# GpSimd products of a selective scan over four quarters at once, halo copies on ScalarE, and new task durations in the planner

## The chip, the core and the metric

The kernel runs on one core of a Trainium2 chip. The core has five engines that work through queues of their own: TensorE (PE, matrix products into PSUM), VectorE (DVE), ScalarE (ACT, functions from tables), GpSimd (POOL) and SyncE (SP, which here issues the DMA transfers). The metric is the device time of one execution in microseconds (us); the median of the runs counts. Traces come from one profiled execution, which has a time of its own.

## The reference

An image batch of 2 x 256 channels x 64 x 64 pixels goes through two residual layers, each after a group normalisation: a Mamba block with a feed-forward part, and attention with 8 heads over all 4096 pixels. The change concerns the scan of the Mamba block:

```python
proj = u @ W_xp.T
dt = softplus(proj[..., :R] @ W_dt.T + b_dt)
Bm, Cm = proj[..., R:R + N], proj[..., R + N:]
A = -exp(A_log)

def step(h, inp):
    dt_t, B_t, C_t, u_t = inp
    dA = exp(dt_t[:, :, None] * A)
    h = dA * h + (dt_t * u_t)[:, :, None] * B_t[:, None, :]
    return (h, einsum('bdn,bn->bd', h, C_t))
```

There are 512 inner channels (DI), N = 16 states for each and R = 16. u is the output of a causal convolution of 4 taps along the pixels and a SiLU. Before the scan stand a layer norm and the input projection; after it a gate, an output projection, a GELU feed-forward layer and the residual sum. All values are 32-bit floats.

## The kernel before

**Tiles and steps.** The Mamba layer comes first, in `mamba_stage`, and the attention follows it. The 4096 pixels of each of the 2 images are cut into 8 tiles of T = 512 columns, so there are 16 tiles. The 512 inner channels are 4 blocks (index k) of 128. A tile's scan has 32 steps: 4 blocks k, times 4 groups of states qd, times 2 values of `quarter` (0 and 2). Rows in a step are 32 channels times 4 states; a block's 128 channels fall into four quarters of 32, and one step handles two of them, j = 0 and 1, that is quarters `quarter` and `quarter + 1`. Two steps that follow each other, with `quarter` 0 and 2, are a pair: all four quarters of one block and one group of states. In all there are 512 steps, 256 pairs and 1024 scan instructions.

**One step** (function `step`, from L808) adds these tasks:

- ACT, twice: `decay` (L828), da = exp(dt * A), into a buffer in SBUF (da0) for j = 0 and in PSUM (da1) for j = 1.
- PE: `broadcast_b`, which spreads the four rows of B over the 128 rows of a PSUM tile bn.
- The product dt*u*B for j = 1, called dbu1 (`times_b`, L834). In three steps of four (`pooled`, g % 4 != 3) it is made by POOL, from dtu_rep and from rows of B in SBUF (rows_b, tile b); in the fourth by DVE, from dtu_rep and bn.
- DVE: the product for j = 0 (L834 too), from dtu_rep and bn, written over bn.
- DVE, twice: `scan` (L839), tensor_tensor_scan of da and the product, starting from `state`, into one half of h.
- ACT: `keep` (L842), a copy of the last column of h into `state`.
- POOL: `times_c` (L845), h times the row of C, 1024 columns wide.
- PE, once a pair: `add_up` (L869, L871) sums h over the states into y; at the last group of states DVE multiplies y by the gate z (L881).

dt and dt*u are made per block k in `softplus` (PE, ACT, DVE, then three POOL instructions of 512 columns at L614, L615 and L617), stored to DRAM, and loaded again spread over the rows as dt_rep and dtu_rep (`load_rep`, L792), two quarters at a time, 512 KB each. The convolution (`conv`) needs the last three columns of the tile before it: POOL copies them from `halo` into xm (L581) and the new ones from xm into `halo` (L583). Around the scan run the work before it for the next tile (`front`), after it for the last (`back`), and from the ninth tile on the attention's projections for the first image (`qkv`).

**What sets the order.** No order is written out by hand. Each task is added to a planner (class `Plan`) with its engine, a due step, a cost in us, what it reads and writes, and for a DMA a time until it lands. `Plan.order` plays all engines forward with these costs: an engine that is free takes the ready task with the smallest due step, if its buffers have room. ACT functions of another table set are ranked 6 steps later (SWITCH), and a table load counts 1.3 us. The order that comes out is emitted and is fixed in the program; on the chip each engine goes through its own list in that order and waits by semaphores. The costs thus change no instruction's length, only the order.

**Buffers.** A `Ring` hands out a number of buffers of one name in turn. `Plan.room` says whether a task's new buffers are free at the planned moment. Of those that matter here there are 4 buffers of two quarters each for dt_rep and for dtu_rep, 3 of da0, 2 of da1, 2 of bn (PSUM), 3 of dbu1, and 5 of h.

Of the kernel before, what the change touches and what calls it, by code (L numbers as in the profile page):

```python
# [107 lines left out]
class Plan:  # L108
# [60 lines left out]
    def room(self, task, now):  # L169
        for buf in task.bufs:  # L170
            ring = buf.ring
            if not ring or buf.given:
                continue
            if not ring.free and len(ring.given) < buf.turn:
                return False
            if len(ring.given) >= ring.bufs:
                old = ring.given[-ring.bufs]
                if old.left or old.free > now:
                    return False
        return True  # L180
# [78 lines left out]
def mamba_stage(ctx, tc, xs, stats_out, consts, w, outs, scratch):  # L259
# [51 lines left out]
    r_dtr, r_dtur = ring("dt_rep", 4, 2, pool=sc), ring("dtu_rep", 4, 2, pool=sc)  # L311
    r_b, r_c = ring("b", NQ, pool=sc), ring("c", NQ, pool=sc)
    r_da0, r_da1 = ring("da0", 3, pool=sc), ring("da1", 2, pool=ps)
    r_bn, r_dbu1 = ring("bn", 2, pool=ps), ring("dbu1", 3, pool=sc)
# [174 lines left out]
    def front(i):  # L489
# [12 lines left out]
        for k in range(KC):  # L502
            add("ACT", due - 41, 0.75, lambda k=k: norm(k), [yn[k], scales_buf[b * KC + k]], [yn[k]])
# [3 lines left out]
        add("PE", due - 40, 1.8, lambda: matmul(mean.tile, [(lnmat, yn.tile[:, k, :]) for k in range(KC)]), [yn], [mean])  # L507
        sq = [Buf(r_tmp) for _ in range(KC)]
        var = Buf(mm)
        for k in range(KC):  # L510

            def centre(k=k):
                nc.vector.tensor_sub(yn.tile[:, k, :], yn.tile[:, k, :], mean.tile)

            add("DVE", due - 39, 0.7, centre, [mean], [yn[k]])
            square = lambda k=k: nc.scalar.activation(sq[k].tile, yn.tile[:, k, :], AF.Square)
            add("ACT", due - 38, 0.65, square, [yn[k]], [sq[k], var] if k == 0 else [sq[k]])
# [6 lines left out]
        add("PE", due - 37, 1.9, lambda: matmul(var.tile, [(lnmat, s.tile) for s in sq]), sq, [var])  # L524
        add("ACT", due - 36, 1.25, rstd, [], [var], ("exp",))
        for k in range(KC):

            def scale(k=k):
                y = yn.tile[:, k, :]
                nc.vector.scalar_tensor_tensor(y, y, gamma[:, k : k + 1], var.tile, ALU.mult, ALU.mult)  # L530

            def shift(k=k):
                y = yn.tile[:, k, :]
                nc.scalar.activation(y, y, AF.Identity, bias=beta[:, k : k + 1])  # L534

            add("DVE", due - 35, 0.75, scale, [var], [yn[k]])
            add("ACT", due - 34, 0.75, shift, [], [yn[k]])
# [19 lines left out]
        add("PE", due - 14, 3.6, project, d.u, [pp, proj, bc])  # L557
        add("ACT", due - 13, 0.6, lambda: nc.scalar.copy(proj.tile[:NP, :], pp.tile[:NP, :]), [pp], [proj])
        add("ACT", due - 13, 0.6, lambda: nc.scalar.copy(bc.tile, pp.tile[:NP, :]), [pp], [bc])
        add("SP", due - 12, 0.4, store_bc, [bc], [d.bc], lands=1.6)  # L560
        add("DVE", due - 12, 0.7, halves, [pp, proj], [proj])
# [4 lines left out]
    def conv(d, b, k, due):  # L566

        px, pc, xm = Buf(mm), Buf(mm), Buf(r_xm, 2)
        h = halo_buf[b * KD + k]

        def project():
            matmul(px.tile, [(w_in[:, c, bass.ts(k, P)], d.yn.tile[:, c, :]) for c in range(KC)])

        def convolve():
            matmul(pc.tile, [(taps[:, k, j, :], xm.tile[:, j : j + T]) for j in range(TAPS)])

        def silu():
            nc.scalar.activation(d.u[k].tile, pc.tile, AF.Silu, bias=conv_b[:, k : k + 1])

        add("PE", due, 1.8, project, [d.yn], [px, xm])  # L580
        add("POOL", due, 0.2, lambda: nc.gpsimd.tensor_copy(xm.tile[:, 0:HALO], halo[:, b, k, :]), [h], [xm[0]])  # L581
        add("ACT", due + 1, 0.6, lambda: nc.scalar.copy(xm.tile[:, HALO:], px.tile), [px], [xm[1]])
        add("POOL", due + 2, 0.2, lambda: nc.gpsimd.tensor_copy(halo[:, b, k, :], xm.tile[:, T:]), [xm], [h])  # L583
        add("PE", due + 2, 3.6, convolve, [xm], [pc, d.u[k]])
        add("ACT", due + 4, 0.6, silu, [pc], [d.u[k]], ("silu",))

    def softplus(d, k, due):
# [22 lines left out]
        add("PE", due, 0.8, lambda: matmul(pd.tile, [(w_dt[:, i, bass.ts(k, P)], d.proj.tile) for i in range(2)]), [d.proj], [pd, dt, lw])  # L610
        add("ACT", due + 1, 1.95, exps, [], [pd, dt], ("exp",))
        add("ACT", due + 1, 1.2, logs, [pd], [lw, w1], ("exp",))
        add("DVE", due + 2, 0.7, rest, [pd], [w1])
        add("POOL", due + 3, 1.27, lambda: nc.gpsimd.tensor_sub(lw.tile, lw.tile, w1.tile), [w1], [lw])  # L614
        add("POOL", due + 3, 1.27, lambda: nc.gpsimd.tensor_add(dt.tile, dt.tile, lw.tile), [lw], [dt])  # L615
        add("SP", due + 3.5, 0.9, lambda: store(d.dt[k], dt, "dt_dram"), [dt], [d.dt[k]], lands=2.0)
        add("POOL", due + 3.5, 1.27, lambda: nc.gpsimd.tensor_mul(lw.tile, dt.tile, d.u[k].tile), [dt, d.u[k]], [lw])  # L617
        add("SP", due + 4, 0.9, lambda: store(d.dtu[k], lw, "dtu_dram"), [lw], [d.dtu[k]], lands=2.0)

    def gate(d, k, due):  # L620
# [7 lines left out]
        add("PE", due, 1.8, project, [d.yn], [pz, z])  # L628
        add("ACT", due + 1, 0.6, lambda: nc.scalar.activation(z.tile, pz.tile, AF.Silu), [pz], [z], ("silu",))

    def back(i):
# [5 lines left out]
        for m in range(KC):  # L637
# [7 lines left out]
            for k in range(0, KD, 2):  # L645
                reads = d.z if k == 0 else d.z[k : k + 2]
                add("PE", due + 2 * m, 1.9, lambda k=k, project=project: (project(k), project(k + 1)), reads, [po])
# [3 lines left out]
                0.7,  # L651
# [7 lines left out]
        for f in range(KH):  # L659
# [8 lines left out]
            add("PE", due + 5 + 1.5 * f, 1.9, up, [yn], [ph, hid if f == 0 else hid[f]])  # L668
            add("ACT", due + 6 + 1.5 * f, 0.7, gelu, [ph], [hid[f]], ("gelu",))
        for m in range(KC):  # L670
# [10 lines left out]
            for f in range(0, KH, 2):  # L681
                reads = [hid, yn[m]] if f == 0 else [hid[f], hid[f + 1]]
                add("PE", due + 19 + 4 * m + f / 2, 2.7 if f == 0 else 1.8, lambda f=f, down=down: down(f), reads, [acc])
# [6 lines left out]
            add("DVE", due + 24 + 4 * m, 1.45, end, [acc], [xt[m], stats_bufs[IMAGES + b][m * NT + t]])  # L690
# [3 lines left out]
    def qkv(b, t, due):  # L694
# [25 lines left out]
        for k in range(KC):  # L720
            add("ACT", due + 2, 0.75, lambda k=k: norm(k), [hid[3 + k], scales_buf[(IMAGES + b) * KC + k]], [hid[3 + k]])
        for n, (i, m) in enumerate(((1, 0), (1, 1), (0, 0), (0, 1))):
# [21 lines left out]
            add("PE", at, 1.8, project, [hid[k] for k in range(5)], [pm, *halves])  # L744
            add("ACT", at + 0.5, 0.7, high, [pm], [hid[5]])
            add("DVE", at + 1, 0.7, low, [pm, hid[5]], [hid[6]])
            add("SP", at + 1.5, 1.7, store, halves, [], lands=3.3)
        for j in range(0, T // P, 2):
# [16 lines left out]
            add("PE", at, 1.8, project, [hid[k] for k in range(5)], [pv, hid[7]])  # L765
            add("ACT", at + 0.5, 0.7, lambda pv=pv: nc.scalar.copy(hid.tile[:, 7, :], pv.tile), [pv], [hid[7]])
# [14 lines left out]
    def pooled(g):  # L781

        return g % 4 != 3

    def load_rep(g, name, src, ring_):

        i, k, _, quarter = where(g)
        rep = Buf(ring_, 2)

        def load():  # L790
            rows = src.tile.rearrange("(c j) t -> c (j t)", j=QUAD)[:, quarter * T : (quarter + 2) * T]
            nc.sync.dma_start(rep.tile, rows.unsqueeze(1).to_broadcast([PQ, QUAD, 2 * T]))  # L792

        add("SP", g - 7, 1.7, load, [src], [rep], lands=3.3)
        return rep
# [13 lines left out]
    def step(g):  # L809
# [4 lines left out]
        if qd == 0:  # L814
            d.dtu_rep[quarter] = load_rep(g, "dtu_rep", d.dtu[k], r_dtur)
            d.dt_rep[quarter] = load_rep(g, "dt_rep", d.dt[k], r_dtr)
# [3 lines left out]
        dt, dtu, rows_b, rows_c = d.dt_rep[quarter], d.dtu_rep[quarter], d.b[qd], d.c[qd]  # L820
        states = [((b * KD + k) * QUAD + quarter + j) * NQ + qd for j in range(2)]
        da = [Buf(r_da0), Buf(r_da1)]
        bn, dbu1 = Buf(r_bn), Buf(r_dbu1)
# [9 lines left out]
        def times_b(engine, out, j, rows):  # L833
            engine.tensor_mul(out.tile, dtu.tile[:, j, :], rows.tile)  # L834

        def scan(j):
            dbu = dbu1 if j else bn
            initial = state[:, b, k, quarter + j, qd : qd + 1]
            nc.vector.tensor_tensor_scan(h.tile[:, j, :], da[j].tile, dbu.tile, initial, ALU.mult, ALU.add)  # L839
# [7 lines left out]
        for j in range(2):  # L847
            add("ACT", g - 6 + j, 0.71, lambda j=j: decay(j), [dt[j]], [da[j]], ("exp",))
        add("PE", g - 6, 0.4, broadcast_b, [d.proj], [bn])
        if pooled(g):  # L850
            add("POOL", g - 6, 1.27, lambda: times_b(nc.gpsimd, dbu1, 1, rows_b), [dtu[1], rows_b], [dbu1])
        else:
            add("DVE", g, 0.7, lambda: times_b(nc.vector, dbu1, 1, bn), [dtu[1], bn], [dbu1])
        add("DVE", g, 0.7, lambda: times_b(nc.vector, bn, 0, bn), [dtu[0]], [bn])
        for j, dbu in ((1, dbu1), (0, bn)):
            add("DVE", g, 1.27, lambda j=j: scan(j), [da[j], dbu, state_buf[states[j]]], [h[j]])
        add("ACT", g - 6, 0.25, keep, [h], [state_buf[at] for at in states])
        add("POOL", g - 4, 2.36, times_c, [rows_c], [h])
# [20 lines left out]
        add("PE", g - 3, 1.9 if qd == 0 else 1.1, add_up, [s.h for s in pair] + ([d.u[k]] if qd == 0 else []), [y])  # L879
        if qd == NQ - 1:  # L880
            add("DVE", g + 2.5, 0.7, lambda: nc.vector.tensor_mul(d.z[k].tile, y.tile, d.z[k].tile), [y], [d.z[k]])  # L881
# [9 lines left out]
    for i, d in enumerate(tiles):  # L891
        d.z, d.b, d.c, d.dt_rep, d.dtu_rep = [], [], [], {}, {}
# [568 lines left out]
```

## Time and profile before

| | |
|---|---|
| median of 3 runs | 4506.31 us (4498.84 to 4507.3) |
| profiled execution, span | 4505.2 us |
| PE busy over the span | 4257.1 us (94%) |
| DVE busy | 3890.9 us (86%) |
| ACT busy | 3768.4 us (84%) |
| POOL busy | 3807.4 us (85%) |
| first and last scan (start) | 96.9 and 2060.8 us |
| first logits of the attention | 2115.5 us |
| activation-table loads, whole program | 332 of 1283 ns |

The span is one execution from its first to its last instruction on the one core. The Mamba layer takes its first 2115.5 us and the attention the rest. In the group lines that follow, a line is: source line, engine, operation, output <- inputs, shape and count, then busy us and mean ns of one instruction, then how long the engine stood idle just before such instructions, and what ended that idle time. Times of instructions that follow each other on an engine overlap a little in the trace, so the distance from one start to the next is somewhat shorter than the duration.

### The profile page before, as it was taken

What the parts mean: (1) busy time and instruction counts of PE and PEld (TensorE: products, weight loads), DVE (VectorE), ACT (ScalarE), POOL (GpSimd) and SP (SyncE); (2) the same over time, 40 slices, a digit from 0 to 9 for tenths busy, and PEclk for the clock granted to TensorE, in tenths of its full rate; (3) what the DMA queues carried; (4) which work ended last, traced back from release to release, by engine and by line L of the source; (5) the groups of instructions that cost most, each with busy time, mean ns of one, the idle gap of its engine ahead of it and who ended that gap; (6) DMA issues with size and microseconds to landing.
All of it is one profiled execution on the core that took longest, in us unless ns stands there. A gap on an engine that the chain in (4) does not pass through costs nothing.

```text
span 4505.2 us, 53942 instructions
## 1 busy us (share of the span) xinstructions
PE 4257.1 (94%) x18530; PEld 1642.2 (36%) x18530; DVE 3890.9 (86%) x3309; ACT 3768.4 (84%) x4842; POOL 3807.4 (85%) x2249
## 2 busy tenths in 40 slices
PE   5789999999999999988999999999999999999998
PEld 2233333333333333333333333333353333333333
DVE  4999999999999989894888888888848888888888
ACT  4788888888788889873999999999849999999997
POOL 2999999999999999994788888888728888888886
PEclk8899999999999999999999999999999999999999
DMA  5233333333443434445210140101091110401100
GB/s 192 94 120 101 110 125 122 127 127 127 143 148 134 139 126 140 147 153 144 58 27 17 29 101 17 26 17 30 24 265 35 46 26 17 101 17 29 27 19 8
DMA packets 172281, 389.23 MB, mean 86 GB/s; under 512 B 23392, under 2 KB 49760, under 8 KB 163808
## 3 DMA queue, kind: packets, MB, share of 16 engines
q1 hardware_dynamic: 171120, 383.37, 27.4%
q8 instruction: 147, 2.41, 0.2%
q10 hardware_dynamic: 880, 2.36, 0.2%
q14 instruction: 134, 1.10, 0.1%
HBM read 292.33 MB, written 93.32 MB: 86 GB/s over the span
## 4 chain that ended last, share of the span: by engine, by line
PE 57%; DVE 4%; ACT 3%; POOL 3%; issue 2%; DMA 1%; DVEq 0%; POOLq 0%; SPq 0%; ACTq 0%
PE s L1131 25%; PE po L1161 24%; PE mm L444 3%; DVE h L839 2%; POOL h L845 2%; ACT da L828 1%; ACT L244 1%; PE mm L677 1%; PE s L1016 1%; PE y L871 1%; POOL dbu L834 1%; PE sums_ps L1212 1%; DVE bn L834 1%; PE mm L641 0%; PE bn L444 0%
## 5 line engine op out<-in xcount | busy, mean ns | idle before, releaser
L1153 DVE TENSOR_REDUCE chunk<-chunk 128x1024 f32<-128x4096 f32 x288 | 1270.6, 4412 | 242.4 <-ACT chunk L1144 242.3
L1194 POOL TENSOR_TENSOR acc_p<-acc_p,e 128x1024 f32<-128x1024 f32 x480 | 1151.9, 2400 | 196.7 <-ACT e L1144 178.0
L1144 ACT ACTIVATE chunk<-s 128x1024 f32<-128x1024 f32 x992 | 1121.5, 1131 | 185.5 <-PE s L1131 139.9
L845 POOL TENSOR_TENSOR h<-h,c 128x1024 f32<-128x1024 f32 x512 | 1208.5, 2371 | 42.0 <-ACT state L842 28.9
L1131 PE MATMUL s<-q,k 128*128 128x512 f32 x4096 | 1228.4, 422 | 5.8 <-ACT chunk L1144 4.9
L1161 PE MATMUL po<-chunk,v 128*32 128x512 f32 x3968 | 1121.7, 642 | 0.0
L1161 PE MATMUL po<-e,v 128*32 128x512 f32 x4224 | 1080.0, 605 | 0.0
L1144 ACT ACTIVATE e<-s 128x1024 f32<-128x1024 f32 x1056 | 1072.7, 1019 | 7.4 <-PE s L1131 6.9
L1131 PEld LDWEIGHTS s<-q,k 128*128 128x128 f32 x4096 | 691.3, 188 | 1014.4 <-issue 915.0
L828 ACT ACTIVATE da<-dt_rep,neg_a 128x512 f32<-128x512 f32 x1024 | 690.5, 701 | 128.7 <-DVE h L839 106.0
L1192 POOL TENSOR_TENSOR acc_p<-acc_p,e 128x512 f32<-128x512 f32 x480 | 620.2, 1292 | 129.3 <-ACT e L1144 106.6
L839 DVE TENSOR_TENSOR_SCAN h<-da,state,dbu 128x512 f32<-128x512 f32 x512 | 650.5, 1273 | 42.8 <-POOL dbu L834 40.2
L839 DVE TENSOR_TENSOR_SCAN h<-da,state,bn 128x512 f32<-128x512 f32 x512 | 647.1, 1264 | 11.6
L834 POOL TENSOR_TENSOR dbu<-dtu_rep,b 128x512 f32<-128x512 f32 x384 | 488.5, 1283 | 19.7 <-DMA dtu_rep<-dtu_dram 15.0
L244 ACT ACT_TABLE_LOAD x332 | 426.0, 1283 | 6.7 <-PEq L1451 0.7
L444 PE MATMUL bn<-proj,pick 112*128 112x512 f32 x512 | 296.4, 595 | 112.2 <-DVE h L839 111.6
L871 PE MATMUL y<-h,sum 128*32 128x512 f32 x2048 | 359.1, 635 | 42.2 <-POOL h L845 42.1
L834 DVE TENSOR_TENSOR bn<-dtu_rep,bn 128x512 f32<-128x512 f32 x512 | 348.6, 681 | 41.4 <-PE bn L444 27.8
L1191 DVE TENSOR_TENSOR acc<-acc,e 128x512 f32<-128x512 f32 x448 | 310.7, 694 | 30.9 <-ACT e L1144 17.5
L1161 PEld LDWEIGHTS po<-chunk,v 128*32 128x32 f32 x3968 | 144.3, 108 | 361.5 <-issue 349.9
L444 PE MATMUL mm<-yn,w_in 128*128 128x512 f32 x512 | 254.7, 625 | 10.3 <-ACT yn L534 9.1
L444 PE MATMUL mm<-yn,w 128*128 128x512 f32 x512 | 246.5, 611 | 4.2 <-ACT hid L666 2.1
(143 smaller groups left out, 4016.3 us busy)
## 6 DMA issues: line engine op xcount, KB each, us to landing
dt_rep<-dt_dram SPq DMA_DIRECT2D x128, 512.0 KB, 5.1
dtu_rep<-dtu_dram SPq DMA_DIRECT2D x128, 512.0 KB, 5.7
k<-qk_dram SPq DMA_DIRECT2D x62, 512.0 KB, 7.3
q<-qk_dram SPq DMA_DIRECT2D x124, 256.0 KB, 4.7
b<-bc_dram SPq DMA_DIRECT2D x64, 256.0 KB, 3.0
c<-bc_dram SPq DMA_DIRECT2D x64, 256.0 KB, 3.7
dt_dram<-dt SPq DMA_DIRECT2D x64, 256.0 KB, 2.0
dtu_dram<-lw SPq DMA_DIRECT2D x64, 256.0 KB, 2.3
```

Of the source, the lines that this page charges most:

```text
L244: self.nc.scalar.preload_act_table_set(self.TABLES[task.table])
L444: nc.tensor.matmul(out, lhsT=lhsT, rhs=rhs, start=(i == 0), stop=(i == len(pairs) - 1))
L828: nc.scalar.activation(da[j].tile, dt.tile[:, j, :], AF.Exp, scale=scale)
L834: engine.tensor_mul(out.tile, dtu.tile[:, j, :], rows.tile)
L839: nc.vector.tensor_tensor_scan(h.tile[:, j, :], da[j].tile, dbu.tile, initial, ALU.mult, ALU.add)
L845: nc.gpsimd.tensor_tensor(h.tile, h.tile, rows_c.tile.unsqueeze(1).to_broadcast([P, 2, T]), ALU.mult)
L1131: nc.tensor.matmul(ps[:, j, :], lhsT=keys[i // NT, kt][:, h, kj : kj + P], rhs=queries[i][:, h, :], start=True, stop=True)
L1144: nc.scalar.activation(e, todo[s].s[half], AF.Exp, scale=SCALE)
L1153: nc.vector.tensor_reduce(out, terms, AX.XY, ALU.add)
L1161: nc.tensor.matmul(tiles[i].po[h * D : (h + 1) * D, :], lhsT=v[:, c, g * P + h * D : g * P + (h + 1) * D], rhs=todo[s].e[h // 2][:, h % 2, :],
L1192: nc.gpsimd.tensor_add(acc_p[:, 1, :], acc_p[:, 1, :], eb[:, 1, :])
L1194: nc.gpsimd.tensor_add(acc_p, acc_p, eb)
```

## The change

1. `pooled` now decides by the pair: 11 of every 16 pairs have their dbu1 products on POOL, spread evenly; before, 3 of 4 single steps had. A pooled pair's two products (quarters 1 and 3) are one POOL instruction of 1024 columns, `both_times_b`, issued in the pair's first step. In the other pairs DVE makes both, one in each step, from bn.
2. So that one instruction can read both quarters, dtu_rep becomes 2 buffers of four quarters (QUAD = 4), filled by two loads of two quarters each, and dbu1 becomes 2 buffers of two products. dt_rep stays as it was. The loads are issued in the order dtu 0 and 1, dt 0 and 1, dtu 2 and 3, then in the next step dt 2 and 3.
3. The two halo copies of `conv` move from POOL to ACT.
4. Nearly all task costs of the planner are replaced by shorter ones.
5. `Plan.room` counts the buffers that a task takes from a ring one by one, so a task that takes two from the same ring is handled.

```diff
     def room(self, task, now):
+        taken = {}
         for buf in task.bufs:
...
-            if not ring.free and len(ring.given) < buf.turn:
+            n = taken[ring] = taken.get(ring, -1) + 1
+            if not ring.free and len(ring.given) + n < buf.turn:
                 return False
-            if len(ring.given) >= ring.bufs:
-                old = ring.given[-ring.bufs]
+            if len(ring.given) + n >= ring.bufs:
+                old = ring.given[n - ring.bufs]
...
-    r_dtr, r_dtur = ring("dt_rep", 4, 2, pool=sc), ring("dtu_rep", 4, 2, pool=sc)
+    r_dtr, r_dtur = ring("dt_rep", 4, 2, pool=sc), ring("dtu_rep", 2, QUAD, pool=sc)
-    r_bn, r_dbu1 = ring("bn", 2, pool=ps), ring("dbu1", 3, pool=sc)
+    r_bn, r_dbu1 = ring("bn", 2, pool=ps), ring("dbu1", 2, 2, pool=sc)
...
-        add("POOL", due, 0.2, lambda: nc.gpsimd.tensor_copy(xm.tile[:, 0:HALO], halo[:, b, k, :]), [h], [xm[0]])
-        add("ACT", due + 1, 0.6, lambda: nc.scalar.copy(xm.tile[:, HALO:], px.tile), [px], [xm[1]])
-        add("POOL", due + 2, 0.2, lambda: nc.gpsimd.tensor_copy(halo[:, b, k, :], xm.tile[:, T:]), [xm], [h])
-        add("PE", due + 2, 3.6, convolve, [xm], [pc, d.u[k]])
-        add("ACT", due + 4, 0.6, silu, [pc], [d.u[k]], ("silu",))
+        add("ACT", due, 0.15, lambda: nc.scalar.copy(xm.tile[:, 0:HALO], halo[:, b, k, :]), [h], [xm[0]])
+        add("ACT", due + 1, 0.49, lambda: nc.scalar.copy(xm.tile[:, HALO:], px.tile), [px], [xm[1]])
+        add("ACT", due + 2, 0.25, lambda: nc.scalar.copy(halo[:, b, k, :], xm.tile[:, T:]), [xm], [h])
+        add("PE", due + 2, 3.44, convolve, [xm], [pc, d.u[k]])
+        add("ACT", due + 4, 0.59, silu, [pc], [d.u[k]], ("silu",))
...
-    def pooled(g):
-
-        return g % 4 != 3
-
-    def load_rep(g, name, src, ring_):
-
-        i, k, _, quarter = where(g)
-        rep = Buf(ring_, 2)
+    def pooled(pair):
+
+        return pair * 11 % 16 < 11
+
+    def load_rep(g, src, rep, at, quarter):
...
-            nc.sync.dma_start(rep.tile, rows.unsqueeze(1).to_broadcast([PQ, QUAD, 2 * T]))
-
-        add("SP", g - 7, 1.7, load, [src], [rep], lands=3.3)
-        return rep
+            nc.sync.dma_start(rep.tile[:, at : at + 2, :], rows.unsqueeze(1).to_broadcast([PQ, QUAD, 2 * T]))
+
+        add("SP", g - 7, 1.7, load, [src], [rep[at], rep[at + 1]], lands=3.3)
...
         if qd == 0:
-            d.dtu_rep[quarter] = load_rep(g, "dtu_rep", d.dtu[k], r_dtur)
-            d.dt_rep[quarter] = load_rep(g, "dt_rep", d.dt[k], r_dtr)
+            if quarter == 0:
+                d.dtu_rep = Buf(r_dtur, QUAD)
+                load_rep(g, d.dtu[k], d.dtu_rep, 0, 0)
+            d.dt_rep[quarter] = Buf(r_dtr, 2)
+            load_rep(g, d.dt[k], d.dt_rep[quarter], 0, quarter)
+            if quarter == 0:
+                load_rep(g, d.dtu[k], d.dtu_rep, 2, 2)
...
-        bn, dbu1 = Buf(r_bn), Buf(r_dbu1)
+        bn = Buf(r_bn)
+        if quarter == 0:
+            d.dbu1 = Buf(r_dbu1, 2)
+        dbu1 = d.dbu1
...
-        def times_b(engine, out, j, rows):
-            engine.tensor_mul(out.tile, dtu.tile[:, j, :], rows.tile)
+        def times_b(j):
+            out = dbu1.tile[:, quarter // 2, :] if j else bn.tile
+            nc.vector.tensor_mul(out, dtu.tile[:, quarter + j, :], bn.tile)
+
+        def both_times_b():
+            odd = dtu.tile.rearrange("p (q j) t -> p j q t", j=2)[:, 1]
+            nc.gpsimd.tensor_tensor(dbu1.tile, odd, rows_b.tile.unsqueeze(1).to_broadcast([P, 2, T]), ALU.mult)
...
         for j in range(2):
-            add("ACT", g - 6 + j, 0.71, lambda j=j: decay(j), [dt[j]], [da[j]], ("exp",))
-        add("PE", g - 6, 0.4, broadcast_b, [d.proj], [bn])
-        if pooled(g):
-            add("POOL", g - 6, 1.27, lambda: times_b(nc.gpsimd, dbu1, 1, rows_b), [dtu[1], rows_b], [dbu1])
-        else:
-            add("DVE", g, 0.7, lambda: times_b(nc.vector, dbu1, 1, bn), [dtu[1], bn], [dbu1])
-        add("DVE", g, 0.7, lambda: times_b(nc.vector, bn, 0, bn), [dtu[0]], [bn])
-        for j, dbu in ((1, dbu1), (0, bn)):
-            add("DVE", g, 1.27, lambda j=j: scan(j), [da[j], dbu, state_buf[states[j]]], [h[j]])
-        add("ACT", g - 6, 0.25, keep, [h], [state_buf[at] for at in states])
-        add("POOL", g - 4, 2.36, times_c, [rows_c], [h])
+            add("ACT", g - 6 + j, 0.63, lambda j=j: decay(j), [dt[j]], [da[j]], ("exp",))
+        add("PE", g - 6, 0.26, broadcast_b, [d.proj], [bn])
+        if not pooled(g // 2):
+            add("DVE", g, 0.6, lambda: times_b(1), [dtu[quarter + 1], bn], [dbu1[quarter // 2]])
+        elif quarter == 0:
+            add("POOL", g - 6, 2.32, both_times_b, [dtu[1], dtu[3], rows_b], [dbu1])
+        add("DVE", g, 0.6, lambda: times_b(0), [dtu[quarter]], [bn])
+        for j, dbu in ((1, dbu1[quarter // 2]), (0, bn)):
+            add("DVE", g, 1.185, lambda j=j: scan(j), [da[j], dbu, state_buf[states[j]]], [h[j]])
+        add("ACT", g - 6, 0.1, keep, [h], [state_buf[at] for at in states])
+        add("POOL", g - 4, 2.32, times_c, [rows_c], [h])
```

The other cost changes have the same form: for PE 1.8 and 1.9 become 1.72, 3.6 becomes 3.44 and the dt projection 0.8 becomes 0.5; for DVE 0.7 and 0.75 become 0.58 to 0.72, 1.45 becomes 1.37; for ACT 0.6 to 0.75 become 0.48 to 0.72, 1.95 becomes 1.76 and 1.2 becomes 0.97; for POOL 1.27 becomes 1.23.

## The prediction

> **What bounds the kernel now.** I read the page first. Its slices show two stages: in slices 2 to 18 all four compute engines are nearly full and the DMA moves 94 to 153 GB/s; from slice 21 on the matrix engine is the fullest at 90% or more. The change touches only the first stage (the Mamba layer), so the share of busy time over the whole span says nothing about it. The tile h of the scan has its first scan at 96.9 us and its last multiplication at 2062.4 us, so the second view is the table of busy time over the stretch from 97 to 2065 us, the scan stretch:
>
> ```profile
> 97.00:2065.00 1968.00, 1800.44 (x5502) 685.22 (x5504) 1822.12 (x1988) 1613.35 (x2673) 1907.63 (x1201) 0.96 0.38 128
> ```
>
> The columns are the stretch, its length, and the busy us of PE, PE weight loads, DVE, ACT and POOL. POOL is busy 1907.6 of 1968 us (96.9%), DVE 1822.1 (92.6%), PE 1800.4 (91.5%), ACT 1613.4 (82.0%). POOL is the bound, but DVE lies only 85 us and PE 107 us below it. That is the main fact of this forecast: whatever is taken off POOL, the next engine catches it after 85 us.
>
> Third, the groups of instructions in that stretch, shapes kept apart (columns: busy us, mean ns of one, idle before it and its releaser):
>
> ```profile
> L845 POOL TENSOR_TENSOR h<-h,c 128x1024 f32<-128x1024 f32 x512 | 1208.5, 2371 | 42.0 <-ACT state L842 28.9 <-issue 5.6 <-DMA b<-bc_dram 2.4
> L839 DVE TENSOR_TENSOR_SCAN h<-da,state,dbu 128x512 f32<-128x512 f32 x512 | 650.5, 1273 | 42.8 <-POOL dbu L834 40.2 <-issue 1.3 <-ACT da L828 0.8
> L834 POOL TENSOR_TENSOR dbu<-dtu_rep,b 128x512 f32<-128x512 f32 x383 | 487.3, 1283 | 13.1 <-DMA dtu_rep<-dtu_dram 8.5 <-DVE h L839 4.6
> L842 ACT COPY state<-h 128x2 f32<-128x2 f32 x512 | 96.1, 189 | 97.6 <-DVE h L839 95.7
> L834 DVE TENSOR_TENSOR dbu<-dtu_rep,bn 128x512 f32<-128x512 f32 x128 | 85.8, 671 | 21.0 <-PE bn L444 20.9
> ```
>
> A POOL product of 512 columns takes 1283 ns and one of 1024 columns 2371 ns, so twice the width is less than twice the time: 2566 against 2371. The same product on DVE takes 671 ns. Fourth, what DVE, soon the fuller engine, waits for in that stretch:
>
> ```profile
> DVE h L839 <- POOL dbu L834: 40.2, 59, 3.6
> DVE bn L834 <- PE bn L444: 27.8, 33, 3.3
> DVE dbu L834 <- PE bn L444: 20.9, 23, 2.2
> DVE hid L734 <- ACT hid L730: 9.2, 10, 1.6
> DVE bn L834 <- DMA dtu_rep<-dtu_dram: 7.6, 7, 2.3
> ```
>
> Only 40 of its 146 idle us (1968 - 1822) are put down to POOL; 49 go to a broadcast of B by PE that came late, the rest to ACT, DMA and small things.
>
> Recorded durations overlap a little: in the order of time a single POOL product starts 1.23 us before the next instruction (1007.24 to 1008.48), a wide one 2.32 (1004.92 to 1007.24), a halo copy 0.15 (1463.08 to 1463.23), a DVE product 0.59 (1011.51 to 1012.11). Busy time of an engine counts overlap once, so I change its sums by these steps.
>
> **What the Trainium skill says.** GPSIMD Engine Reference, section 3.1, puts a two-input tensor_tensor at about 2.6 cycles an element, beside a cost of dispatch for each instruction. The trace agrees: 1088 ns for 512 further columns is 2.12 ns each, which leaves 195 ns fixed, and that is what merging two products saves. ScalarE: Activation LUTs, section "What ACT_TABLE_LOAD costs", has 1283 ns for the load and some 1380 ns of drain, 2.66 us a switch. The trace has the 1283 ns but not the drain: a load at 1500.54 is followed by its activation at 1501.83. I price a load at 1.29 us. SBUF — State Buffer, section "SBUF: two separate sides", says that DVE and GpSimd share a pair of ports, taken for a whole instruction by a DVE operation with two SBUF inputs. The DVE product that becomes more frequent reads B from PSUM (bn), as the present one does, so I add nothing for it; its 671 ns beside a busy POOL shows no blocking.
>
> **The change, part by part, in the scan stretch.**
>
> (1) *Products on POOL.* 16 tiles x 16 pairs of steps = 256 pairs, 11 of 16 pooled: 176 wide instructions in place of 384 single ones. Removed 384 x 1.235 = 474 us, added 176 x 2.32 = 408 us: -66 us of POOL. The shape is that of the product by C, so the price is measured.
>
> (2) *Products on DVE.* 80 pairs x 2 = 160 against 128: +32 x 0.59 = +19 us of DVE.
>
> (3) *Halo copies.* 128 leave POOL: 120 lie in this stretch, 120 x 0.15 = -18 us. On ACT I price them by the nearest row, the two-column state copy, at 0.10 us from start to start when queued (1491.79 to 1491.89) to 0.19 us alone: +13 to +24, say 20 us. ACT is idle 355 us and hides them. They stand in ACT's queue between scan-feeding exponentials, and PE's convolution waits for them; before it waited 19.0 us of weight-load time for POOL's. Cover gone, the cost is at most the 24.
>
> (4) *A new plan.* The instruction order of the two programs has 332 activation-table loads before and 349 after: +17 x 1.29 = +22 us of ACT. With (3), ACT goes to 1655 us, still 313 below the present length. The task costs change too. The old plan thinks DVE the fuller engine: per step 2 x 1.27 + 0.7 + 0.7/4 = 3.42 us of DVE against 2.36 + 0.75 x 1.27 = 3.31 of POOL. The trace has the reverse, about 2 x 1.19 + 0.59 + 0.15 = 3.12 against 2.32 + 0.75 x 1.235 = 3.25. The new plan has 3.16 against 3.12, what (1) and (2) give. I count an order made for the true durations as a reason to expect few new stalls, with no us of its own; unknown, from -20 to +20 us.
>
> (5) *Buffers.* The same bytes of dtu_rep come as two pieces of four quarters instead of four of two. A wide product now waits for both dtu loads of its channel block, and in SP's queue a dt load can stand between them. The least is nothing; the most is one more 512 KB load at each of 16 tile starts, where the chain of waits shows dtu_rep coming last (4.85 us at 1430): some 3 us of transfer each, 48 us. Elsewhere the load is due 7 steps of 3.84 us ahead and lands in 5.7. I take 8 us, inside the idle time chosen below. dbu1 grows from 3 single buffers to 2 pairs, and POOL may run two pairs ahead.
>
> Sums: POOL 1908 - 66 - 18 = 1824; DVE 1822 + 19 = 1841; PE 1800; ACT 1655. DVE is the new bound, POOL 17 and PE 41 us below. The stretch is 1841 plus DVE's idle time. If only DVE's waits for POOL vanish, 146 - 40 = 106 us remain: 1947, a gain of 21. If DVE, as the bound, waits as little as POOL does now (60): 1901, a gain of 67. Part of the other waits are POOL's at second hand: PE works in order and stands 42 us before the sum y, for POOL's h, with the next broadcast of B queued behind it. So I take the middle, 83 us idle: 1924, a gain of 44. Outside the stretch nothing changes: the last tile's back end (2065 to 2115.5, where the first logits start) and the attention do the same work. The profiled execution spans 4505.2 us; minus 44 is 4461. The median of the runs, 4506.3, lies 1 us above it, so I say 4462.
>
> **Rivals.**
>
> *A, the relief passes in full.* The new order, made with true durations, keeps DVE idle for 40 to 60 us: 1891, a gain of 77, 4429. For it: POOL reaches 97% today on a plan with wrong durations. Against: then three engines would be above 95% at once.
>
> *B, another queue sets the pace.* PE has 1800 us of work and stands 112 us more for bn, since the two broadcast buffers are released by DVE's scans; ACT has 42 us more. If PE's in-order stalls stay as they are, DVE keeps 115 us idle: 1956, 4494. For it: the late broadcasts already cost DVE more (49) than POOL does. Against: part of PE's stalls are POOL's.
>
> *C, slower: the wide product comes late.* It must be ready whole for the first of four scans, is 2.32 instead of 1.23 us long, waits for both loads, and only two pairs fit the ring. Today a product delays DVE by 40.2/384 = 0.10 us on average. With DVE's other 106 us kept, it decides from (1968 - 1841 - 106)/176 = 0.12 us a product; at 0.3 us the stretch is 1841 + 106 + 53 = 2000, 4538. Against: in POOL's order, 26 of the 176 wide products stand only one multiplication by C ahead of the step that reads them, 94 two, 48 three and 8 four; before it was 140 of 384 at one, 185 at two, 58 at three. So they are issued earlier, by more than their greater length in most cases (a step is 3.84 us).
>
> *D, it doesn't do what it says:* excluded for the counts, which the order of the built program shows (176 wide, 160 on DVE, no halo copy on POOL).
>
> **How the numbers follow.** My forecast, 4440 to 4488, has 0.55; A 0.20; B 0.13; C 0.12. The range 4430 to 4500 leaves out half of A, nearly all of C and a little of B: two in ten. Under 0.2% (9 us) a measurement of this kernel can't tell from no change. Faster takes the forecast, A and half of B: 0.82; same the rest of B and the edge of C: 0.07; slower 0.11.
>
> **What would show it.** In the changed kernel's stretch POOL should fall to some 1824 us busy and DVE rise to about 1841, the wide row read 176 x 2.37 us, the DVE row 160; DVE at 95 to 96% should be the fullest, and its wait for POOL's dbu below 40 us. The attention, from its first logits to the end, should keep its 2390 us (4505.2 - 2115.5). I am wrong if DVE's waits for dbu grow, or its waits for bn pass 60 us, or ACT, with its added loads, shows up ahead of DVE or PE.

## The result and the profile after

The changed kernel takes 4487.67 us (median of 8 runs, 4486.84 to 4494.86) against 4504.59 us before (8 runs): a ratio of 0.9968, 95% interval 0.9959 to 0.9977. It is faster by 14 us (by the ratio) to 17 us (by the medians), between a third and two fifths of the 44 us forecast, and inside the forecast's range of 4430 to 4500. All medians here are of executions at the usual granted clock; one of the four executions of e8, below, had a clock of 0.69 instead of 0.98, took 5529.7 us, and is left out.

The profiled execution spans 4487.8 us, 17.4 less than before's. The scan stretch (first scan to last multiplication by C) ends at 2057 instead of 2065 us and takes 8 us less. The last tile's back end, from there to the attention's first logits at 2099.6 us, takes 8 us less, and the attention 2388.2 us against 2389.7. Busy time over the stretch, in the columns of before (stretch, length, PE, weight loads, DVE, ACT, POOL):

```profile
97.00:2057.00 1960.00, 1780.18 (x5514) 686.57 (x5516) 1838.73 (x2021) 1646.68 (x2812) 1832.55 (x874) 0.96 0.38 128
```

The forecast's sums of work came out: POOL 1832.6 (1824 forecast), DVE 1838.7 (1841), ACT 1646.7 (1655), PE 1780.2 (1800). POOL, DVE and ACT have the work that was worked out for them, yet the stretch is 1960 us and not 1924. (PE's busy time fell by 20 us though 12 more of its instructions lie in the stretch. Its sums y alone went from 359.1 to 332.9 us with the same 2048 matmuls, so the same work can show a different busy time on PE.) What is different is DVE's idle time: 1960 - 1839 = 121 us, where I had taken 83. The groups that changed, in the same stretch:

```profile
L856 POOL TENSOR_TENSOR h<-h,c 128x1024 f32<-128x1024 f32 x512 | 1203.7, 2366 | 90.7 <-ACT state L853 64.2 <-issue 19.2 <-POOL h L856 5.0
L850 DVE TENSOR_TENSOR_SCAN h<-da,state,bn 128x512 f32<-128x512 f32 x512 | 647.8, 1266 | 29.6 <-ACT halo L585 6.0 <-PE y L882 4.0 <-ACT state L853 1.7
L845 POOL TENSOR_TENSOR dbu<-dtu_rep,b 128x1024 f32<-128x1024 f32 x176 | 416.1, 2364 | 40.6 <-DVE h L850 23.8 <-issue 11.5 <-PE y L882 3.7
L841 DVE TENSOR_TENSOR dbu<-dtu_rep,bn 128x512 f32<-128x512 f32 x160 | 106.5, 666 | 23.5 <-PE bn L446 23.4
L853 ACT COPY state<-h 128x2 f32<-128x2 f32 x512 | 94.9, 188 | 83.5 <-DVE h L850 83.0
```

176 wide products at 2364 ns and 160 products on DVE at 666 ns, as forecast. POOL now stands idle 91 us before its products by C, 64 us of them for the state copy that follows DVE's scans: it waits for DVE. The waits of DVE, the fullest engine now (sum in us, times, longest):

```profile
DVE dbu L841 <- PE bn L446: 23.4, 6, 7.9
DVE h L850 <- POOL dbu L845: 15.4, 11, 2.0
DVE bn L841 <- PE bn L446: 14.1, 22, 1.3
DVE proj L552 <- ACT bc L561: 9.8, 8, 2.5
DVE h L850 <- PE y L882: 8.9, 5, 4.0
DVE h L850 <- ACT halo L585: 6.0, 2, 3.0
```

The waits for POOL's product fell from 40.2 to 15.4 us, 25 us. DVE's whole idle time fell from 146 to 121 us, also 25. Its work rose by 17 us, and 25 - 17 = 8 us is the stretch's gain. So everything outside the waits for POOL stayed as large in sum as it was, 106 us. (The 6.0 us put down to a halo copy are two waits in which a sum y on PE ended 0.1 us before the scan started, at 505.46 and 867.76 us. A scan reads no halo, so PE is the likelier releaser.) The fall of the waits for POOL alone doesn't make a gain either: with the new costs and the old structure they fall to 14.6 us (e7, below), and that kernel is slower than before.

PE's queue shows where some of the relief went. Two groups of its matmuls before and after, in the same form as the other group lines:

```profile
L871 PE MATMUL y<-h,sum 128*32 128x512 f32 x2048 | 359.1, 635 | 42.2 <-POOL h L845 42.1
L444 PE MATMUL bn<-proj,pick 112*128 112x512 f32 x512 | 296.4, 595 | 112.2 <-DVE h L839 111.6
L882 PE MATMUL y<-h,sum 128*32 128x512 f32 x2048 | 332.9, 639 | 15.4 <-POOL h L856 15.0
L446 PE MATMUL bn<-proj,pick 112*128 112x512 f32 x512 | 305.3, 612 | 134.4 <-DVE h L850 133.0
```

PE waits 27 us less for POOL's h, as the forecast had hoped, and 21 us more for DVE to release a buffer of bn. What such waits do can be seen at one place in three tiles, here on DVE (start, duration, then in brackets the idle time before and its releaser):

```profile
1386.51 1.27 DVE L850 TENSOR_TENSOR_SCAN h<-da,state,dbu 128x512 f32<-128x512 f32 x1
1387.70 1.25 DVE L850 TENSOR_TENSOR_SCAN h<-da,state,bn 128x512 f32<-128x512 f32 x1
1396.62 0.69 DVE L841 TENSOR_TENSOR dbu<-dtu_rep,bn 128x512 f32<-128x512 f32 x1 [7.67 <-PE bn L446]
```

and on PE at the same time:

```profile
1382.52 0.80 PE L446 MATMUL bn<-proj,pick 112*128 112x512 f32 x1 [3.05 <-DVE h L850]
1383.11 1.91 PE L880 MATMUL y<-u,diag_d 128*128 128x512 f32 x2
1384.96 1.93 PE L882 MATMUL y<-h,sum 128*32 128x512 f32 x8
1386.82 4.38 PE L446 MATMUL mm<-yn,w 128*128 128x512 f32 x8
1391.04 3.60 PE L446 MATMUL mm<-xm,taps 128*128 128x512 f32 x8
1394.47 1.88 PE L446 MATMUL mm<-yn,w 128*128 128x512 f32 x4
1395.79 0.80 PE L446 MATMUL bn<-proj,pick 112*128 112x512 f32 x1
```

PE first idles 3 us for a bn buffer that DVE has not released, and then runs 13 us of other matmuls before the next broadcast of B, for which DVE waits 7.7 us. DVE makes the products of this pair itself, so both need bn. At this place each of the two engines waits for the other in turn, and the planned order fixes when.

### The profile page after: what moved, and what is told of

Same layout as the page of the kernel before. It is cut to its first block, busy times and chain, and to the rows that moved or that the text cites. A ratio compares the mean times of both kernels' runs of the same rounds, so it can differ in the third digit from the quotient of the medians.

```text
span 4487.8 us, 53634 instructions
## 1 busy us (share of the span) xinstructions
PE 4226.4 (94%) x18530; PEld 1637.2 (36%) x18530; DVE 3906.2 (87%) x3341; ACT 3801.0 (85%) x4987; POOL 3729.1 (83%) x1913
## 4 chain that ended last, share of the span: by engine, by line
PE 61%; DVE 8%; issue 2%; DMA 1%; ACT 1%; POOL 1%; SPq 0%; DVEq 0%; ACTq 0%; POOLq 0%
PE s L1142 25%; PE po L1172 24%; PE mm L446 6%; DVE h L850 5%; PE y L882 1%; DVE bn L841 1%; PE mm L679 1%; PE bn L446 1%; PE s L1027 1%; PE sums_ps L1223 1%; PE mm L643 1%; DMA qk_dram<-chunk 1%; DVE dbu L841 0%; POOL h L856 0%; PE y L880 0%
## 5 line engine op out<-in xcount | busy, mean ns | idle before, releaser
L850 DVE TENSOR_TENSOR_SCAN h<-da,state,dbu 128x512 f32<-128x512 f32 x512 | 643.8, 1270 | 27.2 <-POOL dbu L845 15.4
L845 POOL TENSOR_TENSOR dbu<-dtu_rep,b 128x1024 f32<-128x1024 f32 x176 | 416.1, 2364 | 40.6 <-DVE h L850 23.8
L446 PE MATMUL bn<-proj,pick 112*128 112x512 f32 x512 | 305.3, 612 | 134.4 <-DVE h L850 133.0
L882 PE MATMUL y<-h,sum 128*32 128x512 f32 x2048 | 332.9, 639 | 15.4 <-POOL h L856 15.0
```

Source lines behind the costliest of these rows:

```text
L446: nc.tensor.matmul(out, lhsT=lhsT, rhs=rhs, start=(i == 0), stop=(i == len(pairs) - 1))
L845: nc.gpsimd.tensor_tensor(dbu1.tile, odd, rows_b.tile.unsqueeze(1).to_broadcast([P, 2, T]), ALU.mult)
```

## The experiments

Absolute times are medians in us. "To the change" means against 4487.67. The ratio with its interval is to the kernel before, run on the same chip as the experiment; its own median was 4503.8 to 4505.2 in all sets, so times from different sets compare to within 2 us.

**First set: which engine's work sets the pace of the changed kernel.** Some 50 us of work are taken from one engine at a time, with the order of all else kept. Each leaves out part of the computation, as its text says.

e1, less on DVE:

```diff
-                nc.vector.scalar_tensor_tensor(y, y, gamma[:, k : k + 1], var.tile, ALU.mult, ALU.mult)
+                pass
-            ... lambda: nc.vector.tensor_mul(d.z[k].tile, y.tile, d.z[k].tile) ...
+            ... lambda: None ...
```

> The changed kernel with 58 us less on DVE and every engine's other work in the same order: the layer norm's scaling (32 instructions, 21 us) and the gate's product (64, 37 us) are left out. If DVE sets the pace, as I forecast, the scan stretch shortens by nearly all of it, 40 to 58 us (about 4435 to 4450 us in all). If PE's queue sets the pace, 5 to 20 us. If no engine does and what is left is waits between engines in a fixed order, 15 to 30 us, and no more than for the other engines.

Measured: 4463.45, ratio 0.9912 (0.9895 to 0.9928). 24 us to the change, of 58 removed.

e2, less on PE:

```diff
-            matmul(pc.tile, [(taps[:, k, j, :], xm.tile[:, j : j + T]) for j in range(TAPS)])
+            matmul(pc.tile, [(taps[:, k, j, :], xm.tile[:, j : j + T]) for j in range(2)])
```

> The changed kernel with 55 us less on PE at the same order: two of the convolution's four taps are left out (128 matmuls of 0.43 us). If DVE sets the pace, at most 10 us are gained. If PE's in-order queue does (rival B), 35 to 55 us. If it is waits in a fixed order, 15 to 30 us.

Measured: 4467.35, ratio 0.9919 (0.9903 to 0.9936). 20 us to the change, of 55 removed.

e3, less on POOL:

```diff
-            nc.gpsimd.tensor_tensor(h.tile, h.tile, rows_c.tile.unsqueeze(1).to_broadcast([P, 2, T]), ALU.mult)
+            part = h.tile[:, :, 0:488]
+            nc.gpsimd.tensor_tensor(part, part, rows_c.tile[:, 0:488].unsqueeze(1).to_broadcast([P, 2, 488]), ALU.mult)
```

> The changed kernel with about 52 us less on POOL at the same order: the product by C is taken over 488 of 512 columns (512 instructions, 48 of 1024 elements fewer, 2.12 ns each). If DVE or PE sets the pace, at most 10 us. If the wide products come late (rival C), 30 us or more. If it is waits in a fixed order, 10 to 25 us.

Measured: 4484.62, ratio 0.9956 (0.9940 to 0.9973). 3 us to the change, of some 51 removed.

e4, less on ACT:

```diff
-            nc.scalar.activation(pd.tile, pd.tile, AF.Abs, bias=bias)
-                nc.scalar.activation(y, y, AF.Identity, bias=beta[:, k : k + 1])
+                pass
```

> The changed kernel with about 56 us less on ACT at the same order: the absolute value in the softplus (64, 37 us) and the layer norm's shift (32, 20 us) are left out. If DVE or PE sets the pace, at most 8 us, as ACT has 313 us of idle time. If the 17 added table loads and the halo copies on ACT are what took the gain, 20 us or more.

Measured: 4485.98, ratio 0.9959 (0.9945 to 0.9973). 2 us to the change, of 56 removed.

DVE and PE each give some 40% of what is taken from them, POOL and ACT almost nothing. PE's part is smaller in the scan itself: in e2's trace 5 us are gained before the first scan (92.2 instead of 97.4), and the stretch is 14 us shorter. So neither DVE nor PE is the bound alone: both hold a part of the pace, and POOL and ACT hardly any. (e4 takes out other work than ACT's added table loads and halo copies, so it speaks against a loss by them but doesn't price them.) Leaving out an instruction also removes the waits on it; in e1 these were small: in the changed kernel PE waited 0.7 us for the gate's product and ACT 1.9 us for the scaling. The scan stretch of e1, in the same columns as above, shows what became of the rest:

```profile
95.00:2033.00 1938.00, 1775.22 (x5520) 686.36 (x5521) 1787.59 (x1930) 1643.42 (x2812) 1831.85 (x874) 0.96 0.40 130
```

DVE's work is down from 1839 to 1788 us, and its idle time is up. The line ends at 2033; the last multiplication by C ends at 2030.5, so the stretch proper is 1935 us, 25 less than the change's, and DVE idles 147 us of it instead of 121.

**Second set: the same for the kernel before, and the task costs by themselves.**

e5 and e6 make the edits of e3 and e2 in the kernel before.

> The kernel before, with about 52 us less on POOL at its own order: the product by C over 488 of 512 columns. If POOL alone bound the kernel before, as I read its 96.9% busy, 40 to 52 us are gained. If the pace is shared with DVE and PE at other places of each tile, 10 to 30 us, and then the change's 84 us off POOL could never have brought 44.

Measured: 4464.78, ratio 0.9917 (0.9900 to 0.9933). 39 us of 52.

> The kernel before, with 55 us less on PE at its own order: two of the four taps of the convolution are left out. If POOL alone bound it, at most 8 us are gained. If the pace is shared, 10 to 25 us.

Measured: 4492.61, ratio 0.9976 (0.9965 to 0.9987). 11 us of 55. Its trace, 17 us shorter than before's, gains 8 of them before the first scan (89.2 us instead of 96.9).

Before the change POOL did set most of the pace, three quarters of it, so that premise holds. But e5 is a surprise on another count: 52 us off POOL at the old order is worth more (39) than the whole change, which takes 75 us off POOL and adds 17 to DVE (17 us by the profiles).

e7 puts the new costs into the kernel before, e8 the old ones into the changed kernel:

```diff
-            add("DVE", g, 1.185, lambda j=j: scan(j), ...
+            add("DVE", g, 1.27, lambda j=j: scan(j), ...
...
-            add("POOL", g - 6, 2.32, both_times_b, ...
+            add("POOL", g - 6, 2.36, both_times_b, ...
```

> The kernel before with the new task costs only (halo copies and single products stay on POOL), 4 of the change alone. If an order made for true durations helps by itself, 5 to 20 us faster than before. If the new order is a worse one on the chip, slower than before by 5 to 20 us, and then it is what took the change's gain. If POOL binds, no change within 5 us.

Measured: 4519.57, ratio 1.0034 (1.0020 to 1.0048): slower than before by 15 us.

> The changed kernel with the old task costs (2.36 for the wide product, 0.2 for the halo copies). If the new costs took the gain, this is 15 to 35 us faster than the changed kernel, 4455 to 4475. If they are needed, it is slower than the changed kernel by 5 us or more. If the order matters little, within 5 us of it.

Measured: 4465.77, ratio 0.9918 (0.9898 to 0.9938): 22 us faster than the changed kernel and the fastest complete kernel of this study. Its scan stretch:

```profile
97.00:2031.00 1934.00, 1785.97 (x5514) 686.34 (x5516) 1829.53 (x2020) 1641.64 (x2806) 1831.08 (x874) 0.97 0.39 130
```

The same work on every engine within 10 us, and DVE idle 1934 - 1830 = 104 us instead of 121. Each engine has the changed kernel's instructions; only their order differs, and with it the number of table loads by a few. The four kernels make a square:

| us | old costs | new costs |
|---|---|---|
| old structure | 4503.8 | 4519.6 |
| new structure | 4465.8 | 4487.7 |

The new structure (wide products, 11 of 16 pairs, copies on ACT) gains 38 or 32 us, whatever the costs, and the new costs lose 16 or 22. That looked like the answer: my 44 for the structure nearly right, and the new costs to blame.

**Third set: why would true costs lose?** I supposed that the old costs help by showing DVE as slower than it is. Only some costs are put back, or all are stretched.

```diff
e9   every DVE cost old (product 0.7, scan 1.27, ...), the others new
e10  every PE cost old (broadcast 0.4, products 1.8 and 1.9, ...), the others new
e11  every changed cost x 1.08 (scan 1.28, wide product 2.506, ...)
e12  -add("DVE", g, 1.185, lambda j=j: scan(j), ...
     +add("DVE", g, 1.19, lambda j=j: scan(j), ...
```

> The changed kernel with the old costs for DVE's tasks alone (product 0.7, scan 1.27 and so on), the new ones elsewhere. If the gain of the old costs is DVE's (the plan then thinks DVE slower than it is, so that what DVE reads is put earlier in the other engines' lists), this comes within 8 us of the old costs in full, 4460 to 4476. If the gain comes from other engines' costs or from all being longer, it stays at 4480 to 4495.

Measured: 4547.69, ratio 1.0096 (1.0079 to 1.0112).

> The same with the old costs for PE's tasks alone (0.4 for the broadcast of B, 1.8 and 1.9 for the products). If it is DVE's costs that matter, within 8 us of the changed kernel, 4480 to 4496. If a PE thought slower than it is spaces its long products better, 4465 to 4478.

Measured: 4520.69, ratio 1.0029 (1.0018 to 1.0040).

> The changed kernel with every new cost 8% longer, so the engines' relations are the trace's and only the handover, the table load and the DMA weigh less. If the old costs helped because a plan needs slack everywhere, 4465 to 4478. If what helps is DVE standing out as the slowest in the plan, within 8 us of the changed kernel, 4480 to 4496.

Measured: 4511.76, ratio 1.0016 (1.0010 to 1.0023).

> The changed kernel with the cost of the scan 1.19 instead of 1.185, a change without meaning that still gives another order. If the order is a lottery, it moves by 8 us or more either way; if orders from like costs are alike, it stays within 5 us of 4488.

Measured: 4488.23, ratio 0.9961 (0.9947 to 0.9976).

My theory fell: with DVE's costs alone the kernel is 60 us slower than the changed one, not 22 faster. Neither PE's costs nor slack everywhere explain e8. e12 also disposes of the three long waits shown above. Its order has none of them, as its waits of DVE show (sum in us, times, longest):

```profile
DVE bn L841 <- PE bn L446: 19.6, 19, 2.4
DVE bn L841 <- DMA dtu_rep<-dtu_dram: 15.4, 7, 3.2
DVE h L850 <- ACT da L834: 15.3, 12, 2.3
DVE proj L552 <- ACT bc L561: 9.5, 11, 1.8
DVE h L850 <- PE y L882: 9.2, 9, 4.1
DVE z L892 <- PE y L882: 6.7, 10, 1.6
DVE dbu L841 <- PE bn L446: 6.5, 7, 2.7
```

and yet it takes the same time. The waits for B fell from 37.5 to 26.1 us, but those for the loads of dtu rose from 4.4 to 15.4 and those for da from 5.0 to 15.3. The scan stretch (97 to 2048) is 9 us shorter, and the last tile's back end after it 9 us longer (51.6 instead of 42.6). In this order the holes, however plain, were not worth their length.

**Fourth set: is it the order's scatter?** Small changes without meaning, around the old and the new costs, and the copies alone.

```diff
e13  old costs, but the scan 1.275 instead of 1.27
e14  old costs, each moved at random by up to 3%
e15  new costs, each moved at random by up to 3%
e16  old costs, the halo copies on POOL at 0.2
e17  the kernel before, but the scan 1.275
e18  the kernel before, each cost moved at random by up to 3%
```

> The changed kernel with the old task costs and the scan at 1.275 instead of 1.27. If the old costs as a set give good orders, within 8 us of 4468. If the order is a lottery, it can lie anywhere between 4468 and 4520.

Measured: 4492.94, ratio 0.9972 (0.9961 to 0.9983).

> The changed kernel with every old task cost moved at random by up to 3% either way. If the old costs as a set are better, 4460 to 4478. If the order is a lottery, 8 us or more away from 4468, likely slower.

Measured: 4484.91, ratio 0.9958 (0.9941 to 0.9974).

> The changed kernel with every new task cost moved at random by up to 3% either way, by the same random numbers. If the new costs as a set are worse, 4480 to 4496. If the order is a lottery, 8 us or more away from 4488 either way.

Measured: 4492.33, ratio 0.9970 (0.9959 to 0.9982).

> The changed kernel with the old task costs and the two halo copies on POOL again, at their old cost of 0.2. If POOL still holds a part of the pace, their 18 us cost up to 10 us (4468 to 4478); if POOL is relieved enough by the wide products, within 5 us of 4468. If the order is a lottery, further off than that either way.

Measured: 4487.76, ratio 0.9962 (0.9948 to 0.9976).

> The kernel before with the scan's cost 1.275 instead of 1.27. If its order is a usual one for its structure, 4496 to 4512; then the change's own worth is some 16 us and my 44 was wrong in substance. If its order is a lucky draw, 4515 to 4535, like the 4520 it had with the new costs; then the structure is worth 25 to 40 us, and the draw took the rest.

Measured: 4507.65, ratio 1.0007 (0.9999 to 1.0016).

> The kernel before with every task cost moved at random by up to 3% either way. The same two readings: 4496 to 4512 if its order is a usual one, 4515 to 4535 if it is a lucky draw.

Measured: 4517.07, ratio 1.0027 (1.0019 to 1.0034).

So e8 is one lucky order and not a merit of the old costs: its neighbours lie at 4493 and 4485, the new costs' at 4488 and 4492. The square above was right in its numbers, and its reading was wrong. Orders from costs that differ by 3% or less from the old or the new ones:

| structure | orders tried, us | mean |
|---|---|---|
| before | 4504, 4508, 4517, 4520 | 4512 |
| changed | 4466, 4485, 4488, 4488, 4492, 4493 | 4485 |
| changed, costs further off (e11, e10, e9) | 4512, 4521, 4548 | 4527 |

Between the first two means lie 27 us, and all six orders of the second row are faster than all four of the first. The third row stands outside this comparison, a choice made with its results known. With it the changed structure's mean is 4499, 13 us below before's; e11 and e10 then lie among before's orders or at their end, and e9 is slower than all of them. So the structure is worth some 27 us near these two sets of costs, known to some 10 us at best with so few orders, and no such figure holds for any costs. The pair that was to be compared shows 14 to 17 because before's order lies 8 us below its mean and the changed one's 2 us above.

Three results don't fit a plain lottery, in which any move of the costs draws a new time. e12 and e15 were to move by 8 us or more if like costs gave unlike orders, and they stayed within 5: the new costs' three orders lie close together, and the scatter of 27 us rests on e8 above all. For the kernel before, 4496 to 4512 was to mean a usual order and 4515 to 4535 a lucky one; e17 (4508) says usual, e18 (4517) says lucky. That before's order is lucky is thus not settled. e16 can't price the halo copies: its 4487.8 lies among the changed structure's usual orders.

## Why the prediction was wrong

- *The sums of work* were right to 20 us on each engine and to 9 us for the three that the change touches: the wide product has the duration of the product by C, DVE makes 160 products, and the copies take 182 and 191 ns of ACT each. That they are hidden is not shown (e4 and e16 don't price them).
- *The step that failed* is the last term of the sum, "So I take the middle, 83 us idle: 1924, a gain of 44". Measured: 121 us idle, 1960. In sum, only waits for POOL went, 25 of 40 us, and the 17 us of added DVE work were paid in full. The forecast's own lower case ("If only DVE's waits for POOL vanish", 21 us) was the nearer one and still too high for the stretch.
- *Why it failed*: I let one engine be the bound and hoped that part of its other waits were POOL's at second hand. PE's own waits for POOL did fall by 27 us, but its waits for DVE to release bn rose by 21 (111.6 to 133.0). DVE's waits for bn fell by 11 us (48.7 to 37.5) and its other waits rose by as much. e1 and e2 show that neither DVE nor PE alone sets the pace after the change (24 of 58 and 20 of 55 us), e5 that POOL had three quarters of it before. Why the other waits rose is not shown.
- *Rival B* had 0.13, and its 4494 was nearer than my 4462: PE's stalls on bn did not shrink, and DVE idles 121 us where it said 115. But PE doesn't set the pace by itself: e2 was to give 35 to 55 us in that case and gave 20.
- *Part (4), the order*, was given no time of its own and -20 to +20 us as its range. Orders of one structure differ by up to 27 us here between near-equal costs and by 82 between unlike ones (e8 and e9). That true durations would give "few new stalls" found no support: with the new costs the kernel before was 15 us slower (e7), about as slow as with slightly moved old ones (e18).
- *Rival A* (4429) did not come: the fastest order tried, e8, is 37 us above it. *Rival C* did not happen: the waits for dbu fell to 15.4 us, the longest is 2.0. *The loads of dtu* cost DVE 4.4 us in this order, within the 8 I took, and more in others (15.4 in e12).
- "Outside the stretch nothing changes" was off by 8 us, the last tile's back end; the attention kept its time to 1.5 us, as predicted.

The Trainium skill, Perfetto Trace Analysis, section "Identifying the Most-Contended Engine", says to optimize the engine with the highest occupancy first. That held for the kernel before: POOL at 96.9% returned 39 of 52 us (e5). In the changed kernel DVE at 93.8% and POOL at 93.5% look alike, and one returned 42% of what was taken off it and the other 6%. Occupancy, the busy share of the stretch, no longer told them apart.

What stays open: what makes one order some 20 us better than its neighbours. The number of long waits (e12) and single engines' costs (e9, e10) do not explain it.

## What to carry to other kernels

When several in-order engines are above 90% busy, don't take the next-fullest engine's work as the new floor; take about the same amount from each engine at a fixed order and read how much comes back. Where a planner fixes the order, time a few orders from slightly moved costs before and after a change, and settle beforehand which of them count: their scatter (up to 27 us here, 0.6%) can be larger than the change, and a two-by-two table of single orders can show a clear effect that isn't there.
